# Layer-1 attention of a two-layer decoder: two steps per unit under a fixed TensorE order, transposed probabilities copied on ScalarE, three transpose banks

## The chip, the cores and the metric

The kernel runs on one core of one Trainium2 chip, in one launch. The metric is the device time of that core in microseconds (us), as the median of several executions. A profile is one further execution, recorded instruction by instruction; its span runs from the first to the last instruction.

## The reference

A decoder of two layers works on x (8 batches, 512 tokens, width 256, all float32) and a context of 8 × 64 tokens. Each layer has self-attention, attention with the context and a feed-forward part, each added to x and layer-normalized. The change is about the two attentions of layer 1:

```python
# self-attention of layer 1: 16 heads of 64
q = x @ wq.T;  lat = x @ w_kv_down.T        # lat has width 128
k = lat @ w_k_up.T;  v = lat @ w_v_up.T
q = q * cos + rotate_half(q) * sin;  k = k * cos + rotate_half(k) * sin
out = softmax(q @ k.T / 8 + causal) @ v
x = layernorm(x + out @ wo.T)
# context attention of layer 1: 8 heads of 64; keys and values of x and of the context together
q1, k1, v1 = x @ Wq1, x @ Wk1, x @ Wv1;  k2, v2 = ctx @ Wk2, ctx @ Wv2
out = softmax(q1 @ concat(k1, k2).T / 8) @ concat(v1, v2)
x = layernorm(x + out @ Wo + bo)
```

Layer 0 has self-attention with a decay mask, context attention and a butterfly feed-forward; layer 1 ends in a mixture of eight experts.

## The kernel before, in words

Everything is float32. The five stages follow each other: self-attention of layer 0, its context attention with the butterfly, self-attention of layer 1 (`l1_self`), context attention of layer 1 (`l1_context`), and the experts. The residual stream of all eight batches stays in SBUF as `xs[b]`. P is 128, S is 512, D is 256; NT = 4 blocks of 128 tokens, KC = 2 blocks of 128 channels.

PSUM is split by `psum(name, s, t, o)` (L70) into three kinds of tiles: s tiles of two banks for scores and for q and k, t tiles of one bank for transposes and v, o tiles of one bank for accumulators. From L620 on the split is `psum("b", 2, 2, 2)`: two s tiles (four banks), two t banks, two o banks. A tile of a new pool waits until all users of the pools released before it are done. `evac` (L98) copies a PSUM tile to SBUF, by turns on VectorE (DVE, L102) and on ScalarE (ACT, L104).

**Self-attention of layer 1.** A unit is one pair of heads of one batch: 8 × 8 = 64 units. Its work comes in these pieces:

- `share` (L831), once a batch: transposes x, and computes the latent `lat` into an o tile.
- `q_and_k` (L840): six matmuls of 512 columns into one s tile `s_q` (L844 for q, L845 for k; the trace shows an f32 matmul as two passes, so twice as many). DVE multiplies them by the cosines into `qk` (L849) and by the signed sines into `turned` (L850), and GpSimd (POOL) issues four DMAs that add the 32-row blocks of `turned`, exchanged in pairs, onto `qk` in SBUF (L853). `turned` has two halves used by turns, `qk` two buffers.
- `v` (L857): four matmuls into a t tile (L860), copied to `vc` on ScalarE (L862).
- `l1_scores` (L889): the four row blocks of a unit's causal scores have 128, 256, 384 and 512 columns. `GROUPS` (L870) puts them in three groups, 128 + 256, 384 and 512, each in its own s tile; the two heads of the pair, j = 0 and 1, lie in rows 0 to 63 and 64 to 127 of `qk` (L899). `masked_softmax` (L259) then adds the mask and takes the row maximum on DVE (L265), makes `nm` from it (L275), and takes the exponential with its sum on ScalarE (L277); `scaled` (L883, L885) divides by the sums on DVE.
- `l1_transposes` (L924): six, six and eight transposes of 128 × 128 for the three groups (three or four for each head and t bank, L931), and an `evac` for each head.
- `l1_values` (L945): adds the products with v to the unit's o tile `o_pv` (L955). After a unit's last group `out_done` copies it to `aT`, and after the batch's last unit `project_and_norm` (L224) puts two pieces of output projection (L233) and a normalization in a list that is worked off one piece a step.

`_pipeline` (L32) orders this: in step n it calls each stage for the unit that lies its lag behind n. For `l1_self` (L966) a step is one group of one unit, the lags are 0 (`l1_pre`, which pops the next `q_and_k` or `v` from the list `ahead`), 1 (scores), 3 (transposes) and 4 (values). The lists of instructions are put together from this by a scheduler; only the stages under `tc.manual_schedule(engines={PE})` keep TensorE's order as written, and `l1_self` isn't one of them.

**Context attention of layer 1.** A unit is a pair of heads of one batch (32 units) and has four iterations, one for each block of 128 query rows. `l1x_pre` (L1000), once a unit: q, k and v (L1020, L1027), and once a batch the values of the context, `o_v2` (L1008), for 64 rows. `l1x_scores` (L1037): for each head 512 columns (L1047) and 64 of the context (L1048) into an s tile, maximum on DVE (L1049), exponential on ScalarE (L1050), `scaled`. `l1x_transposes` (L1055): four transposes for each head through `probs_transposed` (L287). `l1x_last_transposes` (L1063): two transposes of the last 64 columns into 64 rows of one t bank, tile `tP2` (L1069), and a copy. `l1x_values` (L1072): values of x (L1081), and at the end those of the context from rows 0 to 63 of `pt2` and `vx` (L1088). Lags are 0, 1, 3, 7 and 3 (L1435), and TensorE's order is written out.

In layer 0, the self-attention loop (L575 to L608) projects q and k three units ahead with `l0_project` (L396), after the four key blocks of a unit; at kt = 3 (and 0) it first works off a piece of `later`, pieces that prepare the next batch or finish the last.

## Time and profile before

| what | value |
|---|---|
| runs of the kernel before | 3712.23, 3716.97, 3719.49 us, median 3716.97 us |
| profiled execution | 3704.71 us, span 3703.0 us, mean granted TensorE clock 0.961 |
| TensorE busy | 3483.6 us, 94% of the span, in 19862 instructions |
| DVE, ScalarE, POOL busy | 2190.3 (59%), 1447.7 (39%), 1091.5 us (29%) |
| stretch 0 to 843 us | layer 0, self-attention: TensorE busy 778.1 us |
| stretch 843 to 1265 us | layer 0, context attention and butterfly: 403.1 us |
| stretch 1265 to 2235 us | layer 1, self-attention: 938.6 us of 970 |
| stretch 2235 to 3132 us | layer 1, context attention: 843.1 us of 897 |
| stretch 3132 to 3703 us | experts: 520.7 us of 571 |

How to read it: a line of a timeline gives the start and length in us, the engine, the line of the code, the operation with output<-inputs, the tile shape of the array (rows*columns), the moving operand (partitions x elements) and how many instructions follow each other (x8). What stands in brackets is the time the engine was idle before, and what ended it. The ends of matmuls are modelled, so lengths overlap by a little; the starts are what to subtract. A line of a waits view has the instruction that waited, what it waited for, us in total, times and the longest. The granted clock is TensorE's, with 1.00 as full speed; the two passes of a float32 matmul count as two instructions.

### The profile page before, as it was taken

The page shows a single profiled execution, that of the slowest core. Times are in us where ns is not written, and L with a number is a line of the kernel's source. Part 1 is how long each engine was busy: PE and PEld are TensorE (multiplying, and loading weights), DVE is VectorE, ACT ScalarE, POOL GpSimd, SP SyncE. Part 2 cuts the span into 40 slices and gives each one's busy share as a digit, 9 for nine tenths or more (in the row PEclk, how much of TensorE's full clock was granted, in tenths as well). Part 3 has the DMA queues.
Part 4 walks back from the last instruction along what each step waited for, and adds up shares of the span by engine and source line. Part 5 has one row for each costly group of instructions (what it writes and reads, how often), then busy time and mean ns, then how long its engine had stood idle before and what let it go on. Part 6 is the DMA issues. An engine that isn't in the chain of part 4 may idle for free. (4 is left out here: it accounts for less than half of the span.)

```text
span 3703.0 us, 53042 instructions
## 1 busy us (share of the span) xinstructions
PE 3483.6 (94%) x19862; PEld 2149.2 (58%) x19862; DVE 2190.3 (59%) x6160; ACT 1447.7 (39%) x2949; POOL 1091.5 (29%) x960
## 2 busy tenths in 40 slices
PE   8999899988999899999999999999999998999995
PEld 3344334446666556665666665555555555888884
DVE  5766777647666377778777775665666655110102
ACT  2444444443333244445444443433334333222222
POOL 3877787751211122222222210010101101222222
PEclk8999999987999999999999999999999999999997
DMA  4100011120000395233222320000000001766674
GB/s 130 30 24 24 24 37 36 35 59 9 4 1 1 84 277 120 35 41 40 37 35 35 41 41 1 6 13 18 18 11 14 18 12 58 241 188 180 185 232 136
DMA packets 165363, 233.94 MB, mean 63 GB/s; under 512 B 26441, under 2 KB 128521, under 8 KB 165106
## 3 DMA queue, kind: packets, MB, share of 16 engines
q1 hardware_dynamic: 138370, 174.78, 15.1%
q0 software_dynamic: 25584, 51.57, 9.4%
q10 hardware_dynamic: 1152, 4.19, 0.3%
q8 instruction: 157, 2.57, 0.3%
q14 instruction: 100, 0.82, 0.1%
HBM read 135.83 MB, written 61.11 MB: 53 GB/s over the span
## 5 line engine op out<-in xcount | busy, mean ns | idle before, releaser
L424 DVE CUSTOM_DVE_ANT_0 scored<-s_sc,decay 128x512 f32<-128x512 f32 x512 | 323.2, 687 | 231.1 <-PE s_sc L419 229.9
L853 POOL DMA_DIRECT2D qk<-turned x256 | 202.8, 1206 | 668.8 <-PE t_v L860 284.1
L477 ACT ACTIVATE pt<-s_st 128x1024 f32<-128x1024 f32 x256 | 261.3, 1024 | 263.0 <-PE s_st L473 232.0
L277 ACT ACTIVATE p<-p,nm 128x128 f32<-128x128 f32 (+3 forms) x512 | 283.1, 554 | 160.4 <-DVE nm L275 157.5
L104 ACT COPY pt<-tP 128x512 f32<-128x512 f32 (+2 forms) x416 | 212.5, 511 | 298.3 <-PE tP L931 196.9
L1050 ACT ACTIVATE p<-s_sc,nm 128x576 f32<-128x576 f32 x256 | 189.7, 743 | 294.6 <-DVE nm L1049 256.5
L885 DVE TENSOR_SCALAR p<-p,rsum 128x576 f32<-128x576 f32 (+4 forms) x768 | 296.2, 427 | 5.5
L1410 DVE TENSOR_SCALAR y<-o_y,share 128x256 f32<-128x256 f32 x71 | 31.4, 480 | 403.6 <-PE o_y L1390 403.6
L1373 PE MATMUL s_h<-xnT,we 128*128 128x256 f32 (+1 forms) x1248 | 262.4, 364 | 1.9 <-DMA we<-in_mo_w 1.9
L102 DVE COPY pt<-tP 128x512 f32<-128x512 f32 (+2 forms) x416 | 248.3, 597 | 14.8 <-PE tP L1069 6.8
L1390 PE MATMUL o_y<-we,h 128*128 128x256 f32 x1136 | 251.6, 379 | 0.0
L265 DVE CUSTOM_DVE_ANT_0 p<-s_sc,tabs 128x128 f32<-128x128 f32 (+3 forms) x512 | 233.0, 484 | 20.7 <-PE s_sc L899 20.7
L1373 PEld LDWEIGHTS s_h<-xnT,we 128*128 128x128 f32 x1248 | 218.1, 193 | 27.1 <-DMA we<-in_mo_w 2.3
L1390 PEld LDWEIGHTS o_y<-we,h 128*128 128x128 f32 x1136 | 215.2, 190 | 28.9
L1411 POOL DMA_INDIRECT total<-y,to x71 | 110.1, 1551 | 397.3 <-DVE y L1410 206.0
L899 PE MATMUL s_sc<-qk 64*128 64x256 f32 (+3 forms) x1024 | 207.8, 477 | 18.3 <-DMA qk<-turned 16.3
L1049 DVE TENSOR_REDUCE nm<-s_sc 128x1 f32<-128x576 f32 x256 | 183.2, 749 | 57.2 <-PE s_sc L1048 56.7
L931 PEld LDWEIGHTS tP<-ident,p 128*128 128x128 f32 x1280 | 137.6, 141 | 127.2 <-issue 59.9
L931 PE MATMUL tP<-ident,p 128*128 128x128 f32 x1280 | 193.9, 284 | 12.0 <-DVE pt L102 8.0
L419 PE MATMUL s_sc<-k,q 32*128 32x512 f32 x1024 | 174.4, 680 | 28.4 <-ACT k L405 26.1
L1216 POOL DMA_INDIRECT rows_in<-z,irow x64 | 63.0, 985 | 451.9 <-DVE hit L1211 349.6
L955 PE MATMUL o_pv<-pt,vc 128*64 128x128 f32 (+1 forms) x2304 | 185.5, 294 | 0.0
(282 smaller groups left out, 6657.1 us busy)
## 6 DMA issues: line engine op xcount, KB each, us to landing
we<-in_mo_w SPq DMA_DIRECT2D x78, 1024.0 KB, 6.1
rows_in<-zero SPq DMA_DIRECT2D x64, 530.0 KB, 11.4
qk<-turned POOLq DMA_DIRECT2D x256, 128.0 KB, 4.5
coef<-in_ff_upw SPq DMA_DIRECT2D x40, 256.0 KB, 3.3
coef<-in_ff_dnw SPq DMA_DIRECT2D x40, 256.0 KB, 3.3
xr<-rows_in SPq DMA_DIRECT2D x32, 265.0 KB, 6.3
x<-in_x SPq DMA_DIRECT2D x8, 512.0 KB, 9.7
total<-x SPq DMA_DIRECT2D x8, 512.0 KB, 2.9
```

Of the source, the lines that this page charges most:

```text
L102: dve.tensor_copy(dst, src)
L104: act.copy(dst, src)
L265: dve.tensor_tensor_reduce(out=p[:, j, 0:n], in0=s[:, j, 0:n], in1=m, scale=1.0, scalar=-3.0e38, op0=op, op1=reduced, accum_out=mx[:, j : ...
L277: act.activation(p[:, j, 0:n], p[:, j, 0:n], AF.Exp, bias=nm[:, j : j + 1], scale=scale, accum_out=sums[:, at + j : at + j + 1],)
L424: dve.tensor_tensor_reduce(out=scored[:, h, :], in0=s[:, j, :], in1=decay[:, i, :], scale=1.0, scalar=-3.0e38, op0=ALU.mult, op1=ALU.max, ...
L477: act.activation(pt, s, AF.Exp, scale=1.0 / 16.0)
L853: pool.dma_start(out=qk[h : h + 32], in_=other[g : g + 32], accum_op=ALU.add)
L885: dve.tensor_scalar(p[:, j, 0:n], p[:, j, 0:n], rsum[:, j : j + 1], None, ALU.mult)
L899: pe.matmul(s[:, j, at : at + n], lhsT=q[h : h + 64, i * P : (i + 1) * P], rhs=k[h : h + 64, 0:n], start=True, stop=True,)
L931: pe.transpose(t[:, n, :], p[:, j, at * P : (at + 1) * P], ident)
L1373: pe.matmul(s[:, j, :], lhsT=w1[:, c, f * P : (f + 1) * P], rhs=xnT[:, c, :], start=(c == 0), stop=(c == KC - 1),)
L1390: pe.matmul(o[:, i, :], lhsT=h[:, f, i * P : (i + 1) * P], rhs=w2[:, f, :], start=(f == 0), stop=(f == 7),)
```

## The change

It touches these places; the names are those of the code above.

1. PSUM pools are made with `reuse_waits="tile"`: a tile waits for earlier users of its own bank only. From `l1_self` on the split is `psum("c", 2, 3, 1)`: three t banks, one o bank. Where there is one o bank, `u_tile` takes a t bank instead, for `o_lat`, `o_out`, `o_k2`, `o_v2`, `o_r`, `o_rank` and `o_y`.
2. `masked_softmax` lets the first DVE operation scale by −1/8 and reduce by minimum, so that it gives `nm` itself; the operation of L275 (256 in the kernel) is gone.
3. `l1_self` has two steps for a unit, scores A (128 + 256 columns) and scores B (384 and 512 columns, still in two s tiles), and TensorE's order is fixed to that written out. `q_and_k` of the next unit is popped in the unit's first step, `v` in its second. Copies of the transposes all go to ScalarE, `pt` has three buffers.
4. `l1_context` transposes the last 64 columns of both heads at once (they lie side by side in `p`, since head 1 has its context columns first), ahead of the other transposes. The context's values are computed for two batches at once on 128 rows, and SP's queue issues two DMAs of 64 rows every second batch that make the copy with the halves exchanged.
5. In layer 0, `l0_project` of three units ahead is called at kt = 3, ahead of the piece of `later`, instead of after the four key blocks.

With these steps and stages `_pipeline` writes TensorE's order of a plain unit u of self-attention as: scores A(u); six transposes of the 384 group of u−1; s_q(u+1); eight transposes of the 512 group of u−1; values of group A of u−1; scores 384 and 512 of u; six transposes of group A of u; t_v(u+1); values of the 384 and 512 groups of u−1; scores A(u+1).

The built programs differ in these counts: TensorE matmuls and transposes 12026 to 11890, copies on DVE 687 to 493 and on ScalarE 716 to 906, DVE operations of tensor and scalar 1412 to 1156, DMAs of SP 388 to 396.

```diff
     @contextmanager
     def psum(name, s, t, o):
+        pool_of = partial(tc.tile_pool, space=PSUM, reuse_waits="tile")
         with (
-            tc.tile_pool(name=f"ps_s{name}", bufs=s, space=PSUM) as pp["s"],
-            tc.tile_pool(name=f"ps_t{name}", bufs=t, space=PSUM) as pp["t"],
-            tc.tile_pool(name=f"ps_o{name}", bufs=o, space=PSUM) as pp["o"],
+            pool_of(name=f"ps_s{name}", bufs=s) as pp["s"],
+            pool_of(name=f"ps_t{name}", bufs=t) as pp["t"],
+            pool_of(name=f"ps_o{name}", bufs=o) as pp["o"],
         ):
+            pp["one"] = o == 1
...
     def o_tile(name):
         return pp["o"].tile([P, 512], F32, tag="o", name=name)
+    def u_tile(name):
+        return t_tile(name).rearrange("p i n -> p (i n)") if pp["one"] else o_tile(name)
...
     def p_tile(n=S, bufs=3):
         return ph.tile([P, 2, n], F32, tag="p", name="p", bufs=bufs)
-    def pt_tile():
-        return ph.tile([P, 2, NT, P], F32, tag="pt", name="pt")
+    def pt_tile(bufs=2):
+        return ph.tile([P, 2, NT, P], F32, tag="pt", name="pt", bufs=bufs)
-    def masked_softmax(s, p, m, n, scale, add_or_mult, sums, at):
-        mx = col("mx", 2)
+    def masked_softmax(s, p, m, n, scale, sums, at):
         nm = col("nm", 2)
-        op, reduced = add_or_mult
         for j in range(2):
             dve.tensor_tensor_reduce(
                 out=p[:, j, 0:n],
                 in0=s[:, j, 0:n],
                 in1=m,
-                scale=1.0,
-                scalar=-3.0e38,
-                op0=op,
-                op1=reduced,
-                accum_out=mx[:, j : j + 1],
+                scale=-scale,
+                scalar=3.0e38,
+                op0=ALU.add,
+                op1=ALU.min,
+                accum_out=nm[:, j : j + 1],
             )
-        dve.tensor_scalar(nm, mx, -scale, None, ALU.mult)
         for j in range(2):
             act.activation(
                 p[:, j, 0:n], p[:, j, 0:n], AF.Exp,
-                bias=nm[:, j : j + 1], scale=scale, accum_out=sums[:, at + j : at + j + 1],
+                bias=nm[:, j : j + 1], scale=-1.0, accum_out=sums[:, at + j : at + j + 1],
             )
...
                         l0_finish(*units[n - 1])
                         if g == 0:
                             later.extend(l0_output(b - 1))
-                elif later:
-                    later.pop(0)()
+                else:
+                    if kt and n + 3 < len(units):
+                        l0_project(*units[n + 3])
+                    if later:
+                        later.pop(0)()
-            if n + 3 < len(units):
-                l0_project(*units[n + 3])
         l0_values(*units[-1], NT - 1)
         l0_finish(*units[-1])
         later.extend(l0_output(NB - 1))
...
             pe.matmul(o[:, f : f + 1], lhsT=bias_row[0:1, f * P : (f + 1) * P], rhs=one, start=True, stop=True)
         dve.tensor_tensor(upb, o[:, 0:8], upb, ALU.add)
-    ctx.enter_context(psum("b", 2, 2, 2))
+    banks = ExitStack()
+    banks.enter_context(psum("b", 2, 2, 2))
     wqT = slot("wqT").rearrange("p (c n) -> p c n", c=KC)
...
         sp.dma_start(out=fills[n], in_=zero.unsqueeze(1).to_broadcast([P, NT, ROW]))
+    banks.close()
+    ctx.enter_context(psum("c", 2, 3, 1))
     def l1_prepare(b, c):
         cols = slice(c * P, (c + 1) * P)
...
     GROUPS = ((0, 1), (2,), (3,))
-    def l1_pre(b, c, m):
-        if (b, c, m) == (0, 0, 0):
-            for _ in range(3):
+    STEPS = ((0,), (1, 2))
+    def l1_pre(b, c, step):
+        for _ in range(2 if (c, step) == (6, 1) else 1):
+            if ahead:
                 ahead.pop(0)()
-        if ahead and (m or c == 7):
-            ahead.pop(0)()
     def scaled(p, sums, n):
...
             dve.tensor_scalar(p[:, j, 0:n], p[:, j, 0:n], rsum[:, j : j + 1], None, ALU.mult)
     put_off = []
+    def groups(stage, some=slice(None)):
+        def run(b, c, step):
+            for m in STEPS[step][some]:
+                stage(b, c, m)
+        return run
     def l1_scores(b, c, m):
         q, k, _ = live["qkv", b, c]
...
         for g, i in enumerate(GROUPS[m]):
             n = (i + 1) * P
             masked_softmax(
-                s[:, :, at : at + n], p[:, :, at : at + n], causal[:, S - n : S], n, 1.0 / 8.0, (ALU.add, ALU.max), sums, 2 * g
+                s[:, :, at : at + n], p[:, :, at : at + n], causal[:, S - n : S], n, 1.0 / 8.0, sums, 2 * g
             )
             scaled(p[:, :, at : at + n], sums[:, 2 * g : 2 * g + 2], n)
             at += n
...
     def l1_transposes(b, c, m):
         p = live.pop(("p", b, c, m))
-        pt = pt_tile()
+        pt = pt_tile(bufs=3)
         order = [at for block in l1_blocks(m) for _, at in block]
         for j in range(2):
             t = t_tile("tP")
             for n, at in enumerate(order):
                 pe.transpose(t[:, n, :], p[:, j, at * P : (at + 1) * P], ident)
-            evac(pt[:, j, 0 : len(order), :], t[:, 0 : len(order), :])
+            act.copy(pt[:, j, 0 : len(order), :], t[:, 0 : len(order), :])
         live["pt", b, c, m] = pt
     def out_done(b, c, o, w, n, plus, then=None):
...
         if m == len(GROUPS) - 1:
             out_done(b, c, live.pop(("o", b, c)), woT1, 8, lambda: xs[b])
-    with phase("l1_self") as ph:
+    with phase("l1_self") as ph, tc.manual_schedule(engines={PE}):
+        for _ in range(3):
+            ahead.pop(0)()
         _pipeline(
-            [(b, c, m) for b in range(NB) for c in range(8) for m in range(len(GROUPS))],
-            [l1_pre, l1_scores, nothing, l1_transposes, l1_values],
+            [(b, c, step) for b in range(NB) for c in range(8) for step in range(len(STEPS))],
+            [
+                (0, groups(l1_scores)),
+                (1, groups(l1_transposes, slice(0, 1))),
+                (0, l1_pre),
+                (1, groups(l1_transposes, slice(1, 2))),
+                (2, groups(l1_values)),
+            ],
             put_off,
         )
...
             return
         if c == 0:
             xT = x_transposed(b)
-            o = o_tile("o_v2")
-            for kc in range(KC):
-                pe.matmul(
-                    o[0:S2, :], lhsT=ctxT[:, kc, b * S2 : (b + 1) * S2], rhs=wv2[:, kc, :], start=(kc == 0), stop=(kc == KC - 1)
-                )
-            vx = work.tile([P, S], F32, tag="lat", name="vx")
-            evac(vx[0:S2, :], o[0:S2, :])
-            live["xT", b], live["vx", b] = xT, vx
+            if b % 2 == 0:
+                o = u_tile("o_v2")
+                for kc in range(KC):
+                    pe.matmul(
+                        o, lhsT=ctxT[:, kc, b * S2 : (b + 2) * S2], rhs=wv2[:, kc, :], start=(kc == 0), stop=(kc == KC - 1)
+                    )
+                vx = [ph.tile([P, S], F32, tag=f"vx{n}", name="vx") for n in range(2)]
+                evac(vx[0], o)
+                for n in range(2):
+                    sp.dma_start(out=vx[1][S2 * n : S2 * (n + 1)], in_=vx[0][S2 * (1 - n) : S2 * (2 - n)])
+                live["vx", b], live["vx", b + 1] = vx, vx[::-1]
+            live["xT", b] = xT
         xT = live["xT", b]
         cols = slice(c * P, (c + 1) * P)
         q, k = qk_tiles()
...
             h = 64 * j
             lhsT = q[h : h + 64, i * P : (i + 1) * P]
             s = s_tile("s_sc").rearrange("p t n -> p (t n)")
-            pe.matmul(s[:, 0:S], lhsT=lhsT, rhs=k[h : h + 64, :], start=True, stop=True)
-            pe.matmul(s[:, S : S + S2], lhsT=lhsT, rhs=k2[h : h + 64, c, b * S2 : (b + 1) * S2], start=True, stop=True)
-            dve.tensor_reduce(nm[:, j : j + 1], s[:, 0 : S + S2], AX.X, ALU.max, negate=True)
-            act.activation(
-                p[:, j, :], s[:, 0 : S + S2], AF.Exp, bias=nm[:, j : j + 1], accum_out=sums[:, j : j + 1]
-            )
+            pe.matmul(s[:, S * j : S * (j + 1)], lhsT=lhsT, rhs=k[h : h + 64, :], start=True, stop=True)
+            at = S - S2 * j
+            pe.matmul(s[:, at : at + S2], lhsT=lhsT, rhs=k2[h : h + 64, c, b * S2 : (b + 1) * S2], start=True, stop=True)
+            s = s[:, at * j : at * j + S + S2]
+            dve.tensor_reduce(nm[:, j : j + 1], s, AX.X, ALU.max, negate=True)
+            act.activation(p[:, j, :], s, AF.Exp, bias=nm[:, j : j + 1], accum_out=sums[:, j : j + 1])
         scaled(p, sums, S + S2)
         live["p", b, c, i] = p
     def l1x_transposes(b, c, i):
-        p = live["p", b, c, i]
+        p = live.pop(("p", b, c, i)).rearrange("p j n -> p (j n)")
         if i == 0:
-            live["pt", b, c] = pts[c % 2], ph.tile([P, 2, S], F32, tag="pt2", name="pt2")
-        pt, _ = live["pt", b, c]
-        probs_transposed(p, [pt[j][:, :, i * P : (i + 1) * P] for j in range(2)], NT)
-    def l1x_last_transposes(b, c, i):
-        p = live.pop(("p", b, c, i))
-        _, pt2 = live["pt", b, c]
-        t = t_tile("tP2")
+            live["pt", b, c] = pts[c % 2], ph.tile([P, S], F32, tag="pt2", name="pt2")
+        pt, pt2 = live["pt", b, c]
+        t = t_tile("tP2")[:, 0, :]
+        pe.transpose(t, p[:, S : S + P], ident)
+        evac(pt2[:, i * P : (i + 1) * P], t)
         for j in range(2):
-            pe.transpose(t[0:S2, j, :], p[:, j, S : S + S2], ident)
-        evac(pt2[0:S2, :, i * P : (i + 1) * P], t[0:S2, 0:2, :])
+            t = t_tile("tP")
+            for k in range(NT):
+                pe.transpose(t[:, k, :], p[:, (S + P) * j + k * P : (S + P) * j + (k + 1) * P], ident)
+            evac(pt[j][:, :, i * P : (i + 1) * P], t)
     def l1x_values(b, c, k):
...
             return
         for j in range(2):
             h = c * P + 64 * j
-            pe.matmul(o[64 * j : 64 * (j + 1)], lhsT=vx[0:S2, h : h + 64], rhs=pt2[0:S2, j, :], start=False, stop=True)
+            pe.matmul(o[64 * j : 64 * (j + 1)], lhsT=vx[j][64 * j : 64 * (j + 1), h : h + 64], rhs=pt2[64 * j : 64 * (j + 1), :], start=False, stop=True)
         def plus():
             xb = work.tile([P, NT, D], F32, tag="att", name="xb")
...
     with phase("l1_context") as ph, tc.manual_schedule(engines={PE}):
         _pipeline(
             [(b, c, i) for b in range(NB) for c in range(4) for i in range(NT)],
-            [(0, l1x_pre), (1, l1x_scores), (3, l1x_transposes), (7, l1x_values), (3, l1x_last_transposes)],
+            [(0, l1x_pre), (1, l1x_scores), (3, l1x_transposes), (7, l1x_values)],
             put_off,
         )
```

More of the change, by code (lines that the diff above doesn't have):

```diff
@@ L228, in piece @@
         def piece(i2):
-            o = o_tile("o_out").rearrange("p (i n) -> p i n", i=2)
+            o = u_tile("o_out").rearrange("p (i n) -> p i n", i=2)
             for j in range(2):
@@ L833, in share @@
             latT = work.tile([P, S], F32, tag="lat", name="lat")
-            o = o_tile("o_lat")
+            o = u_tile("o_lat")
             for k in range(KC):
@@ L989, in decoder_kernel @@
     for c in range(4):
-        o = o_tile("o_k2")
+        o = u_tile("o_k2")
         for kc in range(KC):
@@ L1157, in route_picks @@
         xnT = live.pop(("xnT", b))
-        o = o_tile("o_r")[:, 0 : NT * NE].rearrange("p (i e) -> p i e", e=NE)
+        o = u_tile("o_r")[:, 0 : NT * NE].rearrange("p (i e) -> p i e", e=NE)
         for i in range(NT):
@@ L1197, in route_places @@
         picks, both = live.pop(("picks", b))
-        o = o_tile("o_rank")
+        o = u_tile("o_rank")
         for i in range(NT):
@@ L1386, in moe_down @@
         xr, _, w2, cells = live.pop(("load", n))
-        o = o_tile("o_y").rearrange("p (i n) -> p i n", i=TILES)
+        o = u_tile("o_y").rearrange("p (i n) -> p i n", i=TILES)
         for i in range(size):
```

## The prediction

> **What bounds the kernel now.** I read the cores view (one core, mean clock 0.961), the page's busy times, the stretches by stage, then single units in the timelines, last the waits. TensorE is busy 94% of the span. The change touches the two attentions of layer 1. Their stretches (start:end, length, then busy us of PE, weight loads, DVE, ACT and POOL, granted clock, DMA share, GB/s):
>
> ```profile
> 1265.00:2235.00 970.00, 938.55 (x6133) 589.26 (x6132) 742.66 (x2551) 450.88 (x1328) 217.28 (x271) 0.99 0.41 75
> 2235.00:3132.00 897.00, 843.09 (x4418) 491.01 (x4416) 551.93 (x1324) 345.50 (x816) 83.07 (x76) 0.96 0.04 13
> ```
>
> Self-attention leaves TensorE idle for 31 of 970 us, context attention for 54 of 897. In the first only TensorE's own work, or a new wait, can matter. One plain unit (a pair of heads) of self-attention on TensorE:
>
> ```profile
> 1707.27 1.98 PE L844 MATMUL s_q<-xT,wqT 128*128 128x512 f32 x4
> 1709.09 1.02 PE L845 MATMUL s_q<-lat,kd_ku 128*128 128x512 f32 x2
> 1710.04 0.93 PE L899 MATMUL s_sc<-qk 64*128 64x128 f32 x8
> 1710.90 0.88 PE L931 MATMUL tP<-ident,p 128*128 128x128 f32 x6
> 1711.70 0.87 PE L955 MATMUL o_pv<-pt,vc 128*64 128x256 f32 x8
> 1712.50 1.16 PE L860 MATMUL t_v<-vu,lat 128*128 128x128 f32 x8
> 1713.59 0.92 PE L899 MATMUL s_sc<-qk 64*128 64x384 f32 x4
> 1714.44 1.42 PE L931 MATMUL tP<-ident,p 128*128 128x128 f32 x8
> 1715.78 0.88 PE L955 MATMUL o_pv<-pt,vc 128*64 128x128 f32 x12
> 1716.59 1.13 PE L899 MATMUL s_sc<-qk 64*128 64x512 f32 x4
> 1717.65 0.88 PE L931 MATMUL tP<-ident,p 128*128 128x128 f32 x6
> 1718.46 1.09 PE L955 MATMUL o_pv<-pt,vc 128*64 128x128 f32 x16
> ```
>
> The next s_q starts at 1719.48, so a unit is 12.21 us, and TensorE only stops within the eight transposes (.27, for a transpose bank). Scores use the array as 64*128, values as 128*64, the rest as 128*128: 11 changes of shape in the unit. Now the way of q and k: s_q, two rope products on DVE, four accumulating DMAs from POOL that turn halves, then the scores.
>
> ```profile
> 1712.28 1.22 DVE L850 TENSOR_TENSOR turned<-s_q,tabs 128x1024 f32<-128x1024 f32 x1
> ```
> ```profile
> 1714.02 3.14 POOL L853 DMA_DIRECT2D qk<-turned  x4 [9.07 <-PE t_v L860]
> ```
> ```profile
> DMA to landing us min/median/max: 5.0/5.0/5.0
> ```
>
> The third line is the tile's answer for the fourth DMA alone, issued at 1715.5: it lands at 1720.5, seven us after `turned` ended at 1713.50. Its scores start at 1722.26, 8.76 us after `turned`: 1.7 us to spare. Over all 64 units the medians after the end of `turned` are: issues .53, 1.02, 1.52, 2.02; landings 3.65, 5.09, 6.14 and 7.05; a score that waits starts .14 after its landing. In the first ten units, beside the zero-fill of rows_in, the last landing is near 11.8, and this was seen:
>
> ```profile
> 1322.85 0.48 PE L899 MATMUL s_sc<-qk 64*128 64x128 f32 x2
> 1326.48 1.62 PE L899 MATMUL s_sc<-qk 64*128 64x128 f32 x6 [3.15 <-DMA qk<-turned]
> ```
> ```profile
> 1321.80:1325.20 3.40, 1.54 (x5) 0.48 (x3) 2.37 (x6) 1.13 (x4) 0.00 (x0) 1.00 0.99 259
> 1325.20:1328.60 3.40, 2.12 (x9) 1.50 (x10) 1.58 (x6) 0.00 (x0) 1.76 (x4) 0.50 1.11 321
> ```
>
> The scores waited 3.15 us for the DMA, and the clock of the next stretches was 0.50. In context attention the waits are for copies out of the transpose banks:
>
> ```profile
> PE tP L1069 <- ACT pt L104: 17.6, 50, 1.5
> PE tP L1069 <- DVE pt L102: 10.5, 11, 2.4
> ```
>
> **What the Trainium skill says.** "TensorEngine Tiling (Array Packing)", section "Key Properties": changing the tiling mode drains TensorE. The trace agrees: .09 us at the end of a group and .05 to .10 on the first matmul of the next. "TensorE: Matmul & The Clock Gate", section "Part 1: The HAM clock gate (the "warmup" mystery)": the clock halves after an idle window of some 3.4 us. The trace is harsher: pauses of 3.15 us (at 1323) and 2.15 us (at 1354) were each followed by 6.8 us at half clock, one of 2.46 us (at 1399) by none. "DMA: Bandwidth & Descriptors", section "SWDGE vs HWDGE vs iDMA": accumulation per element comes only with GpSimd's DMAs, so these four can't move to a quicker queue; the same page's "Anatomy of one DMA — SWDGE (gpsimd) path" makes a 128 KB transfer about 2.3 us as an estimate, while the trace has 3.1 us for the quickest and 5.0 for the fourth of a set.
>
> **Self-attention, TensorE's own work.** The pinned order of the new program, a unit u: scores A(u); six transposes of u−1; s_q(u+1); eight transposes of u−1; values A(u−1); scores 384 and 512 (u); six transposes of u; t_v(u+1); values B(u−1); then scores A(u+1). That is 6 shape changes for 11. 5 × .19 = .94 saved, with the .27 wait: 12.21 − .94 − .27 = 11.0 us.
>
> **The new wait.** Before, s_q is issued ahead of the previous unit's scores A, and its own scores come 12 us later. After, s_q(u+1) comes behind scores A(u) and is needed by the very next scores A. s_q ends .86 + .80 + 2.77 = 4.43 us into the unit, `turned` 2.4 us later at 6.83, and TensorE has 11.0 − 6.83 = 4.2 us of work left, where the last landing takes 7.05 and .14. So the unit's length is this loop: from the first score that waits for the last landing, .82 (rest of scores A) + .71 (transposes) + 2.57 + .16 (s_q and its tail) = 4.26; DVE may still be scaling group A, 0 to .2; two rope products 2.36; 7.05; .14. Sum 13.8 to 14.0; I take 14.0. TensorE idles 3.0 of these. Behind the waiting score stand all of TensorE's queue, then ScalarE's copies, and s_q itself, which is why the delay isn't caught up. Two of the eight units of a batch also have an output piece of 7.1 us (32 matmuls × .2155 and the edges), which fills the 3.0: 4.1 each. A batch: 8 × 14.0 + 8.2 + .6 (the latent product, less what it fills) = 120.8, against 115.7 now: +5.1, times 7 = +36. First batch: 112 + 2.6 + 7 units × (11.8 − 7.05) = 148 against 116.7: +31. Together **+67**.
>
> **The clock.** The gap is 1.0 us, one score, then 2. Of the 41 full-clock stretches of 3.4 us in the trace that were idle for 40% or more, 27 were followed by half clock (3.4 us in 20 spells, 6.8 in 14, longer in 7, counting all). Half clock over the loop's TensorE part costs 1.3 us (3.4 long) to 3.0 (6.8, the 4.26 doubled and more): mean 2.0. 64 units less 16 with an output piece = 48 × 2/3 × 2.0 = **+64**; bounds 0 and 48 × 3.0 = 144.
>
> **Copies on ScalarE, three banks, min-reduction.** ScalarE is busy 7.2 us of a unit now and takes three copies of .46 to .57 more: 8.7 of 14, hidden; behind a waiting copy stand exponentials of the same unit, which are due later. DVE loses three copies (.54 to .67) and 256 nm operations of .17: it is busy 10.4 of 12.2 now, and bounds nothing in a 14 us unit. 0, with −5 to +15 if a copy holds an exponential. The third bank is taken from the accumulators; products formerly in o banks go through t banks: 0. scores 512 share a buffer with s_q and wait for the second rope product: 2.36 to 2.4 against 2.65 of work in between: 0, up to .3 × 64 = 19 if alone, but the loop above covers it.
>
> **Context attention.** A plain iteration is 3.60 us of work (scores 1.24, transposes 1.02, values 1.0, last pair .33); measured 3.74 to 3.99. After, one transpose of 128 columns instead of two of 64 saves .11, one shape change fewer .12: 3.37. Its two score buffers go round in 1.3 (scores) + 1.5 (maxima) + .74 (exponential) and tail, 3.5 to 3.75, so 3.6, from 3.88: .28 × 128 = 36. Eight fewer o_v2 matmuls of two passes × .43 = 7, partly in idle time. I take **−40**, −20 to −80 (all 28 us of the bank waits and half of the half-clock time). Eight halves of vx go over SP's otherwise empty queue, needed 30 us later: 0; 2.9 us each if uncovered.
>
> **The rest.** Layer 0's projection goes ahead of the later pieces: TensorE's 26 us of waits for k at 7 batch boundaries may go, but the exponential then stands behind the normalization on ScalarE and ends about when the projection ended: 0, −30 to +5. Bank waits by tile only matter at stage edges: 0 to −3. Experts: TensorE 99% busy, nothing moves: 0.
>
> **The sum.** +67 + 64 − 40 = +91. The profiled execution took 3704.7 (span 3703.0), which would become 3796; the median of the runs is 12 us above it, so 3717 + 91 = **3808**.
>
> **Rivals.** *The DMA doesn't bind (faster).* If the last landing came within 4.2 us of `turned` instead of 7.05, the unit would be 11.0 and small waits, 11.25: 64 × .96 = 61; 3717 − 61 − 40 = 3616. For it: the quickest landing of a DMA alone is 3.1 us, and zero-fill traffic and DVE lie beside the sets I measured. Against: steady units without zero-fill show 7.05 again and again, and issues alone take 2.0. Chance .17. *The wait binds, the clock holds:* the gap is cut in two by a score, and a 2.46 us pause cost nothing: 3717 + 67 − 40 = 3744, .20. *Half a wait, and more from context attention:* landings near 5.7, clock held, −60 there: 3717 + 33 − 60 = 3690, .08. That the order isn't what is said is excluded: it is written out in the built program.
>
> **How the numbers follow.** The forecast has .55, its own range 3755 (clock 32, context −60) to 3880 (clock 115, context −20 and 5 more of small waits). The range 3680 to 3880 leaves out the first rival and .03 above. About 0.2%, 7 us, is what a measurement of this kernel can tell from no change. Faster: .17 + .06 = .23; same: .05 from the edges of the second and third rivals; slower .72.
>
> **What would show it.** Plain units of 14 us with a wait of scores on qk<-turned of 1 and 2 us in each; clock digits of 7 to 8 through self-attention; context iterations near 3.6 without waits of transposes on banks. Units near 11.2 and no DMA wait would prove the main step wrong; a full clock beside the waits only the second.

## The result, and the profile after

The changed kernel takes 3819.97 us, the median of 4 runs (3805.48 to 3831.93), against 3714.6 (3707.37 to 3719.49) for the kernel before in the same comparison: 1.029 of it, with a 95% interval of 1.025 to 1.032. It is slower by 105 us. The profiled execution took 3805.48, with a span of 3803.8 and a mean granted clock of 0.946.

The stretches of the changed kernel by stage (start:end, length, busy us of PE, weight loads, DVE, ACT and POOL, granted clock, DMA share, GB/s), self-attention and context attention of layer 1:

```profile
1264.00:2361.00 1097.00, 946.30 (x6131) 629.15 (x6130) 648.75 (x2092) 517.26 (x1519) 216.48 (x266) 0.93 0.37 66
2361.00:3240.60 879.60, 836.53 (x4276) 505.97 (x4274) 548.50 (x1346) 338.10 (x817) 85.29 (x78) 0.95 0.05 17
```

TensorE was idle for 31 us of self-attention before and is for 151 of it now, and the clock there fell from 0.99 to 0.93. Taken between the first instructions of the stages in both traces, layer 0 gained 3.1 us, self-attention lost 128.4 (967.9 to 1096.3), context attention gained 25.2 (905.1 to 879.9), and the experts lost 0.6: +100.8, the difference of the spans. (The stages run from the first s_q, s_qk and expert matmul.)

One plain unit of self-attention on TensorE, from the timeline (start, length, line, operation, tile shape, operand, count, and the idle time before with what ended it; the x4 and x2 of s_q are the six passes of its three matmuls):

```profile
1627.97 0.46 PE L917 MATMUL s_sc<-qk 64*128 64x128 f32 x2 [0.53 <-DMA qk<-turned]
1629.92 0.89 PE L917 MATMUL s_sc<-qk 64*128 64x128 f32 x6 [1.50 <-DMA qk<-turned]
1630.74 0.88 PE L949 MATMUL tP<-ident,p 128*128 128x128 f32 x6
1631.45 1.88 PE L853 MATMUL s_q<-xT,wqT 128*128 128x512 f32 x4
1633.17 1.02 PE L854 MATMUL s_q<-lat,kd_ku 128*128 128x512 f32 x2
...
1641.92 0.46 PE L917 MATMUL s_sc<-qk 64*128 64x128 f32 x2 [0.53 <-DMA qk<-turned]
1643.84 0.89 PE L917 MATMUL s_sc<-qk 64*128 64x128 f32 x6 [1.47 <-DMA qk<-turned]
```

From 1627.97 to 1641.92 is 13.95 us, where a unit took 12.21. Scores A wait twice for qk<-turned, once for each pair of DMAs. On DVE the second rope product, and on POOL the DMAs that follow it:

```profile
1635.52 1.21 DVE L859 TENSOR_TENSOR turned<-s_q,tabs 128x1024 f32<-128x1024 f32 x1
```
```profile
1637.26 3.14 POOL L862 DMA_DIRECT2D qk<-turned  x4 [10.80 <-PE s_sc L917]
```

`turned` ends at 1636.73 and the score that needs the last landing starts at 1643.84, 7.1 us later. The landings are as before: medians after `turned`, without the first ten units, 3.65, 5.09, 6.12 and 7.06 us, against 3.64, 5.08, 6.10 and 7.04. No DMA got slower; TensorE now comes back to them before they are done. The waits view of TensorE in this stage:

```profile
PE s_sc L917 <- DMA qk<-turned: 115.3, 75, 11.7
PE s_sc L917 <- DVE turned L859: 16.7, 36, 1.9
```

In context attention the waits of transposes on banks (17.6 and 10.5 us in the kernel before) are gone from the list. What is left at its head:

```profile
PE s_qk L1051 <- ACT p L1084: 9.7, 3, 3.7
...
PE s_sc L1079 <- DVE k L1054: 6.3, 6, 1.1
```

### The profile page after: what moved, and what is told of

Read it like the earlier page. It is cut to its first block, busy times and chain, and to the rows that moved or that the text cites. A ratio compares the mean times of both kernels' runs of the same rounds, so it can differ in the third digit from the quotient of the medians.

```text
span 3803.8 us, 52783 instructions
## 1 busy us (share of the span) xinstructions
PE 3483.8 (92%) x19718; PEld 2200.9 (58%) x19718; DVE 2091.0 (55%) x5710; ACT 1505.2 (40%) x3139; POOL 1093.9 (29%) x960
## 5 line engine op out<-in xcount | busy, mean ns | idle before, releaser
L917 PE MATMUL s_sc<-qk 64*128 64x256 f32 (+3 forms) x1024 | 219.4, 491 | 137.6 <-DMA qk<-turned 115.3
L950 ACT COPY pt<-tP 128x384 f32<-128x384 f32 (+1 forms) x384 | 182.7, 510 | 332.6 <-PE tP L949 332.0
L949 PEld LDWEIGHTS tP<-ident,p 128*128 128x128 f32 x1280 | 153.0, 149 | 116.6 <-issue 103.6
L917 PEld LDWEIGHTS s_sc<-qk 64*128 64x128 f32 x1024 | 93.1, 196 | 206.8 <-issue 129.7
L1079 PE MATMUL s_sc<-k,q 64*128 64x512 f32 x512 | 197.7, 657 | 11.6 <-DVE k L1054 6.3
```

The costliest lines, as they stand in the source:

```text
L917: pe.matmul(s[:, j, at : at + n], lhsT=q[h : h + 64, i * P : (i + 1) * P], rhs=k[h : h + 64, 0:n], start=True, stop=True,)
L949: pe.transpose(t[:, n, :], p[:, j, at * P : (at + 1) * P], ident)
L1079: pe.matmul(s[:, S * j : S * (j + 1)], lhsT=lhsT, rhs=k[h : h + 64, :], start=True, stop=True)
```

## The experiments

Theory 1: self-attention lost its time because s_q, the rope products (the two DVE products with the cosines and sines) and the turning DMAs now lie between two successive scores A. The lead below is the time from s_q to the scores that use it. Theory 2: the fixed order, the copies on ScalarE or the banks cost it. All ratios are to the kernel before, run beside the kernel on the same chip (medians of before: 3709.85 to 3718.04).

**Lead given back, first way.** Layer 1 issues four pieces ahead instead of three; nothing else.

```diff
-        for _ in range(3):
+        for _ in range(4):
             ahead.pop(0)()
```

> The changed kernel with one edit: four pieces instead of three are issued ahead of self-attention, so that TensorE does s_q of unit u+2 in the second step of unit u, a whole unit and more before its scores. Theory 1 (the time was lost because s_q, the rope products and the turning DMAs lie between two successive scores A): the waits of scores on qk<-turned vanish outside the zero-fill, a plain unit takes 11.0 to 11.4 us instead of 13.95, self-attention falls from 1096 to about 900 us, the clock there returns to 0.98 or more, and the whole kernel is near 3625 us, faster than the kernel before. Theory 2 (the fixed order, the three copies on ScalarE or the bank split of two score tiles and one accumulator cost the time): units stay at 13 us or more and the kernel above 3750 us.

Measured: 3705.66 us, ratio 0.9975 (0.9956 to 0.9994). The waits for the DMA fell from 115 to 18 us, all in the zero-fill, but self-attention took 998 us instead of some 900, in plain units of 12.31 and 12.91, and the kernel missed the 3625 us expected. The timeline shows a new wait:

```profile
1716.24 0.87 PE L949 MATMUL tP<-ident,p 128*128 128x128 f32 x6
1716.95 1.06 PE L869 MATMUL t_v<-vu,lat 128*128 128x128 f32 x8
1717.85 0.60 PE L949 MATMUL tP<-ident,p 128*128 128x128 f32 x4
1719.55 0.66 PE L949 MATMUL tP<-ident,p 128*128 128x128 f32 x4 [1.10 <-ACT pt L950]
```

With one more piece ahead, t_v and s_q exchange places, and the rope products come on DVE ahead of the maxima of scores A. The second copy of a pair stands on ScalarE behind the exponentials of group A, which wait for these maxima; the transposes wait for that copy's bank (75 us in the stage). So theory 1 holds for the DMA, and the number failed because this edit moves more than the lead.

**The DMAs left out.** The loop with the four accumulating DMAs is taken out; q and k lack the part with the sine.

```diff
-            for h in range(0, P, 32):
-                g = h ^ 32
-                pool.dma_start(out=qk[h : h + 32], in_=other[g : g + 32], accum_op=ALU.add)
             live["qk", b, c] = qk
```

> The changed kernel without the four accumulating DMAs of a unit: the turned halves are computed by the same DVE product but not added, so q and k lack the sine part. TensorE's order, copies, banks and buffers are those of the changed kernel. Theory 1: scores A then wait at most for the rope products of DVE; a plain unit is 11.0 to 11.4 us, the whole kernel 3610 to 3640 us. Theory 2 (order, copies, banks): units stay near 14 us. If the rope products or the shared score buffer bind next, units lie between, near 12.

Measured: 3629.34 us, ratio 0.976 (0.974 to 0.977); plain units 11.43 us, self-attention 909.2. Order, copies and banks are those of the changed kernel, and with them the stage is 59 us faster than before. They aren't the loss.

**Lead given back, second way.** The list of pieces is put together so that s_q is that of unit u+2 and stays in its place between the transposes; t_v is that of u+1 still.

```diff
-            qk = ph.tile([P, 2, S], F32, tag="qk", name="qk", bufs=2)
+            qk = ph.tile([P, 2, S], F32, tag="qk", name="qk", bufs=3)
...
-        return ([share] if c == 0 else []) + [q_and_k, v]
-    ahead = [piece for b in range(NB) for c in range(8) for piece in l1_prepare(b, c)]
+        return share, q_and_k, v
+    made = [l1_prepare(b, c) for b in range(NB) for c in range(8)]
+    ahead = [made[0][0], made[0][1], made[0][2], made[1][1]]
+    for n in range(len(made)):
+        if n + 2 < len(made):
+            ahead.extend(made[n + 2][0:2] if (n + 2) % 8 == 0 else made[n + 2][1:2])
+        if n + 1 < len(made):
+            ahead.append(made[n + 1][2])
```

(The four first pieces are popped ahead of the stage, and the two that begin a batch together.)

> The changed kernel with its order of kinds of work on TensorE, but the s_q between the two sets of transposes is that of unit u+2 instead of u+1 (three buffers for qk instead of two); t_v stays that of u+1. So DVE and ScalarE do the same in the same places, only the DMAs have a whole unit more. Theory 1 (the short lead of the turning DMAs alone made the loss): a plain unit takes 11.4 to 11.5 us, as without the DMAs, no score waits for qk<-turned, self-attention takes 905 to 925 us and the kernel 3625 to 3645 us. Theory 2 (a lead given back only shows a second limit at once, ScalarE's copies behind exponentials, which held the run with four pieces ahead at 12.3 and 12.9 us): units of 12.3 or more, kernel near 3700.

Measured: 3634.52 us, ratio 0.979 (0.975 to 0.983), self-attention 926.4, plain units 11.43 us as without the DMAs. In the timeline scores A no longer wait, and their eight matmuls stand in one line:

```profile
1714.47 1.13 PE L923 MATMUL s_sc<-qk 64*128 64x512 f32 x4 [0.17 <-DVE turned L859]
...
1717.22 1.75 PE L979 MATMUL o_pv<-pt,vc 128*64 128x128 f32 x28
1718.90 0.93 PE L923 MATMUL s_sc<-qk 64*128 64x128 f32 x8
```

This version beats both kernels: 185 us under the changed one, for one more buffer and another list. Order, copies and banks stayed and the loss is gone: theory 1 holds.

**The loop made longer.** s_q moves behind the eight transposes and the values of group A.

```diff
-                (0, l1_pre),
                 (1, groups(l1_transposes, slice(1, 2))),
                 (2, groups(l1_values)),
+                (0, l1_pre),
```

> The changed kernel with s_q of the next unit moved later in TensorE's order by eight transposes and the values of group A (1.8 us), nothing else. Theory 1 (a loop from the last landing through s_q, the rope products and the DMAs to the next scores): a plain unit grows by 1.6 to 1.8 us, to about 15.7, and the kernel by 80 to 110 us, to about 3915. If TensorE's own work, ScalarE or DVE set the unit, nothing changes: 3820 within 10.

Measured: 3924.27 us, ratio 1.057 (1.0535 to 1.0605), 104 us over the changed kernel. Between the second scores of successive units, plain units at full clock take 15.9 to 16.1 us (15.7 expected), those with a spell of half clock about 17.5.

**The pauses filled.** Transposes of the identity ahead of scores A keep TensorE busy while it would wait: 24 in every unit, then 22 in all but the two units of a batch with an output piece.

```diff
+        if m == 0:
+            for _ in range(24):
+                pe.transpose(s[:, 0, 0:P], ident, ident)
```

> The changed kernel with 24 additional 128-column transposes of the identity into the score tile ahead of each unit's scores A (2.6 us of TensorE work that nothing reads; 64 times 2.6 = 167 us of it). Theory 1 with its second part (the pauses let the clock be halved): the extra work lies inside the wait for the last landing, plain units stay at 14.0 to 14.2 us, the clock in self-attention returns to 0.98 or more, and the kernel gets faster by 40 to 70 us, to about 3765. If the pauses cost nothing through the clock: 3820 us within 10. If TensorE's work and not the wait sets the unit: about 3980 us.

```diff
-        if m == 0:
-            for _ in range(24):
+        if m == 0 and not (b and c in (1, 2)):
+            for _ in range(22):
```

> The changed kernel with 22 additional transposes of the identity ahead of scores A, read by nobody, in all units but the two of a batch that hold an output piece. If the halved clock after the pauses costs what the run with 24 in all units points to (1120 us less 16 units of 2.8 and 64 of .25 is 1059, 37 less than 1096): plain units 14.0 to 14.2 us, clock in self-attention 0.97 or more, kernel 3775 to 3795. If it costs the 64 of the prediction: near 3756. If it costs nothing: 3820 or a little above.

Measured: 3830.58 us, ratio 1.030 (1.028 to 1.032), and 3816.59, ratio 1.027 (1.024 to 1.030). Time at half clock in self-attention fell from 150 to 48 and 61 us, and plain units stayed at 14.2 and 13.98: that much was as expected, the time was not. The units, measured from second score to second score, say why (mean in us of batches 2 to 7, by place in the batch; places 0 and 1 hold the output pieces, place 6 the next batch's latent product):

```
place in the batch        0      1      2      3      4      5      6      7    sum
before                 18.85  20.09  12.45  12.22  12.22  12.22  16.11  11.96  116.1
changed                20.18  18.10  17.14  13.96  14.95  14.31  16.15  14.45  129.2
24 in every unit       21.24  20.87  14.78  14.42  14.29  14.29  17.97  14.93  132.8
22 in some units       18.88  18.10  18.22  14.08  14.09  14.01  17.74  14.74  129.9
s_q two units ahead    18.53  18.10  15.04  11.43  11.43  11.43  16.30  11.43  113.7
```

The filling in some units saves 1.3 us at place 0 and 0.9 and 0.3 at places 4 and 5, where a spell of half clock had fallen on s_q. It costs 1.1 and 1.6 at places 2 and 6, whose next scores A had little or nothing to wait for, and 0.3 at place 7. (In every unit, it costs 2.8 at place 1 behind an output piece.) The sums of the changed kernel and of the filling in some units are alike by cancellation, so the runs can't give the price of the clock by their totals. By place it is read from the changed kernel: units in which no spell of half clock lies on the loop take 18.7, 18.1, 16.4, three times 13.95, about 15.3, and 13.8, 124.1 in sum; the mean is 129.2. At place 2 all seven later batches have a spell, but in five of them it comes after `turned`, and the landings end the unit all the same, at 16.4 to 16.7 us. So the clock costs about 5 us a batch, 35 in seven: an estimate from these units. One such spell, in the stretches and in the timeline of the changed kernel:

```profile
1754.80:1758.20 3.40, 1.40 (x12) 0.81 (x8) 1.38 (x3) 0.14 (x1) 0.00 (x0) 1.00 0.48 69
1758.20:1761.60 3.40, 3.40 (x10) 2.24 (x10) 1.85 (x12) 2.27 (x10) 0.00 (x0) 0.50 0.00 0
```
```profile
1758.33 1.54 PE L949 MATMUL tP<-ident,p 128*128 128x128 f32 x6
1759.67 2.84 PE L853 MATMUL s_q<-xT,wqT 128*128 128x512 f32 x4
```

After a stretch with TensorE busy for 1.40 of 3.40 us, the six transposes and the q part of s_q take 1.34 and 2.67 us from start to start, instead of .71 and 1.72 in the unit above.

**The order left to the scheduler.** The changed kernel without the fixed order.

```diff
-    with phase("l1_self") as ph, tc.manual_schedule(engines={PE}):
+    with phase("l1_self") as ph:
```

> The changed kernel without the fixed order of TensorE in self-attention; the scheduler then places the six transposes and s_q of the next unit mostly behind the first score of scores A, ahead of the others. Theory 1 (loop): s_q no longer stands behind the wait for the last landing but only behind that for the second one, which comes 2 us earlier, and its 3.5 us of work lie in the gap: the loop is 0.2 + 0.8 + 2.7 + 2.4 + 5.2 = 11.3 us, TensorE's work 11.4 with two to four more shape changes of .19; a plain unit 11.7 to 12.2 us, kernel 3650 to 3690. If the short lead costs by itself, wherever s_q stands: 13.5 us or more, kernel above 3780.

Measured: 3741.81 us, ratio 1.008 (1.006 to 1.011), plain units mostly 12.7 us; self-attention 1032.8. Direction right, number missed. A unit in the timeline:

```profile
1751.21 0.46 PE L917 MATMUL s_sc<-qk 64*128 64x128 f32 x2 [1.22 <-DMA qk<-turned]
1751.60 0.87 PE L949 MATMUL tP<-ident,p 128*128 128x128 f32 x6
1752.31 1.88 PE L853 MATMUL s_q<-xT,wqT 128*128 128x512 f32 x4
1754.03 1.02 PE L854 MATMUL s_q<-lat,kd_ku 128*128 128x512 f32 x2
1754.98 0.92 PE L917 MATMUL s_sc<-qk 64*128 64x128 f32 x6
...
1758.90 1.13 PE L917 MATMUL s_sc<-qk 64*128 64x512 f32 x4 [0.33 <-DVE turned L859]
```

s_q is out of the shadow of the last landing, so the short lead costs far less than with the fixed order, 78 us less. But `turned` ends 3.8 us after s_q and not 2.4. On DVE:

```profile
1755.09 1.23 DVE L858 TENSOR_TENSOR qk<-s_q,tabs 128x1024 f32<-128x1024 f32 x1 [4.18 <-PE s_q L854]
1756.23 0.28 DVE L270 CUSTOM_DVE_ANT_0 p<-s_sc,tabs 128x128 f32<-128x128 f32 x1
...
1757.55 1.20 DVE L859 TENSOR_TENSOR turned<-s_q,tabs 128x1024 f32<-128x1024 f32 x1
```

The maxima of scores A stand between the two rope products, 1.3 us that my sum lacked: 3.8 (first score to the end of s_q) + 3.8 + 5.1 (second landing) = 12.7, the unit measured. The first batch, beside the zero-fill, takes 141 us here and 98 with s_q two units ahead: there the short lead still costs.

**Copies, banks, context attention.** Five runs take these parts singly. First, s_q two units ahead with copies by turns on DVE and ScalarE:

```diff
-            act.copy(pt[:, j, 0 : len(order), :], t[:, 0 : len(order), :])
+            evac(pt[:, j, 0 : len(order), :], t[:, 0 : len(order), :])
```

> The run with s_q two units ahead, with the copies of self-attention's transposes by turns on DVE and ScalarE again instead of all on ScalarE. DVE is busy some 9.4 us of an 11.43 us unit there and would get 1.5 copies on average, 0.9 us, more. If the move to ScalarE is needed in this order: DVE is late with maxima and scaling, units of 11.7 to 12.3 us, kernel 3650 to 3690. If it makes no difference: 11.43 us, 3634.

Measured: 3636.78 us, ratio 0.980 (0.977 to 0.982), units 11.28 and 11.43. The second case came, 3634: from 1400 to 2100 us DVE is busy 551 us instead of 491, ScalarE 331 instead of 393, and neither binds. Moving the copies makes no difference in this order.

Then the same version with two transpose banks and two accumulators in self-attention:

```diff
-    banks.close()
-    ctx.enter_context(psum("c", 2, 3, 1))
...
     # after self-attention
+    banks.close()
+    ctx.enter_context(psum("c", 2, 3, 1))
```

> The run with s_q two units ahead, with two transpose banks and two accumulator banks in self-attention (three and one from context attention on). From the trace of that run: t_v starts 0.7 us after the six transposes of group A, and with two banks it would have to wait until ScalarE has copied the first of them, about 0.4 us; all other banks are copied in time. So plain units of 11.7 to 12.0 us and a kernel near 3660. If the third bank matters here as in context attention (1.2 us for each block of rows there, with packed transposes): units above 12.5, kernel above 3700. If it does nothing: 11.43 and 3634.

Measured: 3677.41 us, ratio 0.989 (0.985 to 0.992), units 11.99 us, the kernel 17 us over the 3660 expected. The wait is where it was expected, t_v on a copy (27.8 us in the stage), and transposes wait on copies for some 15 us more; the third bank in place of a second accumulator is worth some 40 us here.

Last, the changed kernel with the self-attention of before (its pipeline, copies, and two and two banks), and context attention in two variants besides:

```diff
-    with phase("l1_self") as ph, tc.manual_schedule(engines={PE}):
...
+    with phase("l1_self") as ph:
+        _pipeline(
+            [(b, c, m) for b in range(NB) for c in range(8) for m in range(len(GROUPS))],
+            [l1_pre, l1_scores, nothing, l1_transposes, l1_values],
+            put_off,
+        )
+    banks.close()
+    ctx.enter_context(psum("c", 2, 3, 1))
```

> The changed kernel with layer 1's self-attention as before (three steps a unit, order left to the scheduler, copies by turns, two transpose banks and two accumulators there, two buffers for pt); context attention, its three banks, layer 0 and the softmax as changed. Theory 1 with the stages read from the two traces (self-attention +128, context attention -25, layer 0 -3): about 3689 us, faster than before by 0.5 to 1%. If the gain of context attention depends on the new self-attention or is a chance of one profile: 3710 to 3720.

```diff
-    ctx.enter_context(psum("c", 2, 3, 1))
+    ctx.enter_context(psum("c", 2, 2, 2))
```

> As the run with the self-attention of before, but with two transpose banks and two accumulators in context attention and the experts too. If the third bank ended the waits of the transposes on copies (28 us in the kernel before): these waits stay, context attention is 10 to 25 us longer than with three banks, kernel 3700 to 3715. If it was the packed transposes alone: 3689 as with three banks.

```diff
-            [(0, l1x_pre), (1, l1x_scores), (3, l1x_transposes), (7, l1x_values)],
+            [(0, l1x_pre), (1, l1x_scores), (3, l1x_transposes), (7, l1x_values), (3, l1x_last_transposes)],
```

(with the functions of context attention of before)

> The run with the self-attention of before and three transpose banks in context attention, with context attention's transposes as before too (two of 64 columns after the others, o_v2 once a batch). So the third bank alone. If it ends the waits on copies (28 us before) and packing adds 29 us of TensorE's time: kernel near 3695. If the third bank is all of the gain: 3665 to 3675, as with packed transposes. If it gives nothing without packing: 3710 to 3720.

```
context attention    two banks             three banks
transposes as before 905.1 (before)        909.5: 3695.54, 0.996 (0.9945 to 0.997)
packed               983.9: 3783.85,       880.9: 3669.46, 0.987 (0.985 to 0.990)
                     1.018 (1.016 to 1.021)
```

The first number of each is the stage in the profile, then median and ratio; the three runs also have the changed layer 0, pools and softmax. By the stage, packing on two banks loses 79 us (66 by the medians), the third bank without packing loses 4, and both together gain 24 (49 by the medians). Of the 25 us between 24 and 49 some 4 lie in the other stages; 20 come from the profiled executions, which lie closer together than the medians (3704.71 with a median of 3718.04 for the kernel before, 3676.14 with 3669.46 for both together). In which stage these 20 lie isn't known. Without packing, the kernel hit the 3695 expected, but not for the reason given: in its profile self-attention, whose pipeline is that of before, was 15 us shorter and context attention 4 us longer. The stretches of context attention, before and with the third bank alone:

```profile
2235.40:3140.40 905.00, 844.19 (x4421) 491.45 (x4420) 557.22 (x1348) 347.83 (x819) 84.92 (x78) 0.96 0.04 15
2218.40:3127.90 909.50, 864.43 (x4422) 511.81 (x4421) 558.13 (x1349) 346.95 (x819) 85.87 (x78) 0.94 0.05 15
```

TensorE's idle time falls from 61 to 45 us, but its busy time grows by 20 us, and the time at half clock from 78 to 101. So the bank ended waits, and this execution lost them again at a lower clock; whether the bank brought that about isn't shown. With packing and two banks the waits view has

```profile
PE tP L1093 <- ACT pt L110: 81.1, 64, 2.6
PE tP L1093 <- DVE pt L108: 60.2, 53, 2.6
```

since an iteration fills three t tiles in a row there. I had expected 10 to 25 us for the two banks and was far off; with both together I had expected 3689, 20 us above what was measured.

## Why the prediction was right

The result, 3820, is 12 us over the forecast of 3808, and the case that happened is the one given the largest chance: the wait binds and the clock falls. That step was right in kind and size. Three other terms were off in opposite directions, the batch 20 us too low, context attention 15 us too good and the clock some 29 us too dear, so that the sum came this close is partly luck.

- **TensorE's own work**: 11.0 us of work forecast, 11.43 measured without the DMAs, .16 of it a wait for `turned`. A little low, since the five changes of shape saved were worth some .13 us each and not .19 (an estimate: 12.21 − .27 less 11.43 − .16, by five); it doesn't set the unit.
- **The loop**: 14.0 forecast, 13.95 measured, and a longer loop made longer units. With the lead given back the wait was gone. The step was right, place and size; only the two waits in a unit are .53 and 1.47 us, where 1 and 2 were forecast.
- **The batch**: 120.8 forecast, 124.1 at full clock, so seven batches are +56 (against 116.1) instead of +36. The mis-sized term is that of the special units: the third took 16.4 and not 14.0. It follows the second output piece, DVE has the normalization to do besides its maxima, `turned` comes late, and the scores of 512 columns wait up to 1.9 us for it (the row `<- DVE turned` in the waits above). First batch: 148 forecast, 149.8 measured, from 116.4.
- **The clock**: +64 forecast, about 35 measured. The mis-sized term is the count: 48 × 2/3 = 32 spells were forecast; after the first batch there are 22, of which the five at place 2 that the wait for the landings hides cost nothing, and 35/17 is about 2 us for each of the others, as forecast. In the first batch none showed beside the DMA's wait (149.8 against the 148 forecast without the clock). The granted clock of the stage is .93, and not the 7 to 8 tenths named as a sign. The page "TensorE: Matmul & The Clock Gate" of the Trainium skill, section "Part 1: The HAM clock gate (the "warmup" mystery)", puts the drop after at least one idle window of some 3.4 us; here two pauses of .53 and 1.47 us with one score between them were enough in some units and not in others.
- **Context attention**: −40 forecast; −25 by the stages of the two profiles. The mis-sized term is that of the plain iteration, 3.88 to 3.6 forecast: of the 58 iterations in which TensorE does nothing else, those under 5 us took 3.87 in the mean before and 3.70 after. 22 of these 51 took 3.38, the 3.37 of TensorE's work in the prediction, the others mostly 3.8 to 4.3. The time at half clock rose besides, from 78 to 90 us in the stage. And the reason was incomplete: neither packing nor the third bank alone shortened the stage.
- **The rest at nothing**: layer 0 −3.1, experts +0.6; copies on ScalarE 0, as far as the order with s_q two units ahead shows it (with four pieces ahead a copy behind exponentials did cost time). The third bank's 0 in self-attention wasn't tried in this order; with s_q two units ahead the bank is worth some 40 us.

First rival (the DMA doesn't bind, 3616): its price was good, 3629 and 3634 in the two runs in which the DMAs don't bind; its premise was wrong, and that of the third rival (landings near 5.7) too, since the landings came at 7.06 us again. Second rival (the clock holds, 3744): less the 35 us of the clock the result would be some 3785, an estimate, since the batch was forecast too low.

## What to carry to other kernels

When an order is made tighter, count for each operand how much work now lies between its issue and its use, and set that against its measured way from end to end, engines and landings together: here, after `turned`, 5.1 us of work (7.1 less the waits of .53 and 1.47) against 7.1. A producer that stands behind its own consumer's wait turns latency into a loop that repeats in every unit; issuing it one unit earlier took one more buffer and gave 185 us. Two edits can each be worth little or be harmful alone and good together (packed transposes and a third bank), so test them as pairs.

## What the runs showed of the hardware

- The landings of four accumulating DMAs of 128 KB after their source is written were the same to .05 us in four kernels of quite different order (before, changed, and both with the lead given back), 3.65, 5.08, 6.1 and 7.05, once the zero-fill was over; beside it the last landing came at some 10 to 14 (medians of the first eight units).
- Half clock for 3.4 us on the loop cost about 1.5 us here (units of 15.3 to 15.6 instead of 13.95); where the spell came after `turned` and the landings ended the unit, five times, it cost nothing that shows (16.4 to 16.7 us all the same).
